# Three mixed inputs' last addition on GpSimd, first products split by token halves, and constants' transfers in the plan of an RWKV-6 block

## The chip, the cores and the metric

The kernel runs on one core of a Trainium2 chip. The metric is the device time in microseconds of one execution, from the runs without a profiler; one further execution was profiled, and all rows below come from it. A core has five engines that run beside each other, each in the order of its own instruction queue: TensorE (PE, matrix products into PSUM), VectorE (DVE), ScalarE (ACT), GpSimd (POOL) and SyncE (SP, which here issues most DMAs).

## The reference

One RWKV-6 block over x of shape (32, 128, 512): batch 32, 128 tokens, 512 channels, 32 heads of 16. Cut to what matters:

```python
xn = ln(x)*ln1_w + ln1_b
sx = previous_token(xn) - xn
xxx = tanh((xn + sx*maa_x) @ maa_w1)            # 512 -> 5 x 32
xxx = matmul(xxx.reshape(b, l, 5, 1, 32), maa_w2)  # each 32 -> 512
x5 = xn + sx*(maa_stack + xxx)                  # five mixed inputs
w = exp(-exp(time_decay + tanh(x5[1] @ decay_w1) @ decay_w2))  # 512 -> 64 -> 512
r, k, v = x5[3] @ Wr.T, x5[0] @ Wk.T, x5[2] @ Wv.T
g = silu(x5[4] @ Wg.T)
# per head and token: out = r . (u*k*v + s);  s = k*v + w*s
x = x + (group_norm(out) * g) @ Wo.T
# second half: ln, token shift, x + sigmoid(xr @ Wr2.T) * (relu(xk @ Wk2.T)**2 @ Wv2.T)
```

All of it is fp32.

## The kernel before

The batch is cut into 8 groups of 4 sequences, so that a group has N = 512 token columns; channels stand in four slices of 128 partitions (NE = 4). For each group the work is written as several Python generators, each a stream of instructions in order:

- `front_mix`: load x, layer norm and transposition (`layernorm_T`), the first product with `maa_w1` (`pm` for inputs 0 to 3, 128 weight columns; `pm2` for input 4), tanh, and for each of five inputs m the products with `maa_w2` (`side_by_side`) and the mixing (`mixed`): one instruction that adds `maa_stack` and multiplies by sx (L453), and one that adds xn (L455), for each of the four slices.
- `front_proj`: the decay product `pd` with `decay_w1` (L489), its tanh (L492), the decay w, and the projections k, r, v, each from one mixed input. `front_gate` makes the gate from input 4.
- `prep` and the `rec_*` streams: the recurrence. For each of 34 steps per group, 32 of them go through POOL (product L689, pair sum L693), DVE (scan L711, product with r L713) and PE (accumulation by transposing products L746). The two others need neither POOL nor the scan.
- `back`: group norm, output projection, second layer norm and the feed-forward part. The last group's `back` runs as two halves (`last1`, `last2`).

No stream waits in Python for the hardware. A planner (`Plan`) draws up one order for all engines ahead of time: each `yield Op(engine, us, ...)` states what the next instructions cost, what they read, write and allocate, and the planner picks, among the streams whose next Op could start within `EPSILON` of the earliest, the one with the earliest due time. A stream's due times run evenly from v0 to v1 over its steps, both from the table `DUE`, with the group's number added. The instructions are then issued in that order, so that an engine's queue holds instructions of several groups, and an instruction whose operands come late holds up everything behind it on its engine. The hardware's own semaphores secure the data; costs and due times only set the order. `xfer` is the planned transfer time on an issuing engine's queue; `port=True` says that an instruction takes the port that DVE and POOL share.

The products with few weight columns: `pm2` multiplies 96 columns of `w1_sb`, of which the middle 32 are zero and the last 32 a copy of the first, so that one tanh (L445) fills both halves of `thb` that `side_by_side` reads with two 64-row weights at once. `pd` likewise has the 64 decay columns twice. The copies are made on POOL in group 0 (L427, L428).

`constants()` issues the small loads at the start of group 0: `vec`, `pv`, `w1_sb`, `w2p`, `dw1_sb`, `dw2p` and `u_sb`, on SP's and ACT's queues, and four small POOL instructions that wait for `vec`. The planner knows nothing of them. The PSUM tiles named `ps` have four buffers, for all streams.

Of the kernel before, what the change touches and what calls it, by code (L numbers as in the profile page):

```python
# [8 lines left out]
F32 = mybir.dt.float32  # L9
I32 = mybir.dt.int32  # L10
AF = mybir.ActivationFunctionType
ALU = mybir.AluOpType
AX = mybir.AxisListType

P = 128
B, L, E = 32, 128, 512
H, S = 32, 16
NE = E // P
HE = P // S
GB = 4  # L20
NG = B // GB
N = GB * L
# [19 lines left out]
WINDOW, KEEP, WAKE = 3.41, 0.4, 0.7  # L42
LANDING = 2.0
HOP = (0.2, 0.05, 0.05, 0.04, 0.08)
EPSILON = 0.0397


DUE = {"rec": (-0.0, 1.1), "mix": (-1.199, -0.678), "proj": (-1.193, 1.513), "gate": (1.096, 1.348), "prep": (0.06, 0.276), "back": (1.128, 2.553), "last1": (-13.962, -9.529), "last2": (6.538, 25.524)}


class Buf:
# [130 lines left out]
def rwkv6_block(ctx: ExitStack, tc: tile.TileContext, x, prev, s0, vecs, u, maa_w1, maa_w2,  # L182
# [44 lines left out]
    u_sb = const.tile([P, S], F32, name="u_sb")  # L227


    w1_sb = const.tile([P, NE, 7 * XM], F32, name="w1_sb")  # L230
    w2p = const.tile([P, 5, E // 2], F32, name="w2p")
    dw1_sb = const.tile([P, NE, 2, XD], F32, name="dw1_sb")
    dw2p = const.tile([P, E // 2], F32, name="dw2p")
    thb = Buf(const.tile([P, N], F32, name="thb"))
    ident = const.tile([P, P], F32, name="ident")
# [4 lines left out]
                          ident.rearrange("p (b h e) -> p b e h", b=GB, e=NE))  # L240
    nc.gpsimd.memset(mhalf, -0.5)
    nc.gpsimd.memset(thb.t, 0.0)
    nc.gpsimd.memset(w1_sb[:, :, 5 * XM : 6 * XM], 0.0)
    nc.vector.memset(w2p, 0.0)

    def constants():
        nc.sync.dma_start(out=vec, in_=vecs)
        nc.gpsimd.tensor_scalar(ffn[:, 0, :], vec[:, V_FK, :], -1.0, 1.0, ALU.mult, ALU.add)
        nc.gpsimd.tensor_scalar(ffn[:, 2, :], vec[:, V_FR, :], -1.0, 1.0, ALU.mult, ALU.add)
        nc.gpsimd.tensor_tensor(ffn[:, 1, :], ffn[:, 0, :], vec[:, V_LN2B, :], ALU.mult)  # L250
        nc.gpsimd.tensor_tensor(ffn[:, 0, :], ffn[:, 0, :], vec[:, V_LN2W, :], ALU.mult)
        nc.sync.dma_start(out=pv, in_=prev)
        halves = lambda w, h: w.rearrange("r (f h p) -> h r f p", h=2, p=P)[h]
        nc.sync.dma_start(out=w1_sb[:, :, 0 : 5 * XM], in_=maa_w1.rearrange("(c p) o -> p c o", p=P))
        for m in (1, 0, 2, 3, 4):
            for h, queue in enumerate((nc.sync, nc.scalar)):
                r = h * XD + (XM if m in (1, 3) else 0)
                queue.dma_start(out=w2p[r : r + XM, m, :].rearrange("r (f p) -> r f p", p=P),
                                in_=halves(maa_w2[m * XM : (m + 1) * XM, :], h))
            if m == 1:  # L260
                nc.sync.dma_start(out=dw1_sb[:, :, 0, :], in_=decay_w1.rearrange("(c p) o -> p c o", p=P))
                for h, queue in enumerate((nc.sync, nc.scalar)):
                    queue.dma_start(out=dw2p[h * XD : (h + 1) * XD, :].rearrange("r (f p) -> r f p", p=P),
                                    in_=halves(decay_w2, h))
        for e in range(NE):
            nc.sync.dma_start(out=lanes(u_sb, e), in_=u[e * HE : (e + 1) * HE, :].unsqueeze(0).to_broadcast([GB, HE, S]))
# [6 lines left out]
    def col(v, e):  # L273
        return vec[:, v, e : e + 1]

    def bt(ap):
        return ap.rearrange("p (b t) -> p b t", t=L)
# [106 lines left out]
    def row(xnT, e, shift, bs=range(GB)):  # L384

        return xnT[:, e * GB + bs[0] : e * GB + bs[-1] + 1, shift : shift + L]

    def matmuls(p, w, xin, e, cols=slice(0, N)):
        for c in range(NE):
            nc.tensor.matmul(p, lhsT=w[:, c, e * P : (e + 1) * P], rhs=xin[:, c, cols], start=(c == 0), stop=(c == NE - 1))  # L390

    def side_by_side(pp, w, up, low):

        for p, h, t in zip(pp, (slice(0, XD), slice(XD, P)), (up, low)):
            nc.tensor.matmul(p.t, lhsT=w[h, :], rhs=t[h, :], start=True, stop=True)  # L395
# [11 lines left out]
    def front_mix(g, d):  # L407

        xt = yield from load_x(g, (lambda: "x1" in data[g - 3]) if g > 2 else (lambda: "xin" in data[0]) if g else None)
        if g == 0:  # L410
            constants()
        need = (lambda: "ln2" in data[g - 3]) if g > 2 else None
        def use(xnT, e, pt, tiles):

            yield Op(ACT, 0.75, w=[(pt, None)])
            nc.scalar.activation(pt.t, pt.t, AF.Identity, bias=col(V_LN1B, e), scale=col(V_LN1W, e))
            sx, xin = tiles
            yield Op(DVE, 0.69, r=[(xnT, e), (xnT, "p"), (pt, None)], w=[(sx, e)])
            nc.vector.tensor_tensor(bt(sx[:, e, :]), row(xnT, e, 0), bt(pt.t), ALU.subtract)
            yield Op(DVE, 0.75, r=[(pt, None), (sx, e)], w=[(xin, e)], end=[pt])  # L420
            nc.vector.scalar_tensor_tensor(xin[:, e, :], sx[:, e, :], col(V_MAAX, e), pt.t, ALU.mult, ALU.add)

        xnT, sx, xin = yield from layernorm_T(g, xt, None, V_LN1W, V_LN1B, 0, use, ("sx", "mx"), need)
        d["xin"] = True
        if g == 0:
            yield Op(POOL, 0.9)
            nc.gpsimd.tensor_copy(w1_sb[:, :, 6 * XM : 7 * XM], w1_sb[:, :, 4 * XM : 5 * XM])  # L427
            nc.gpsimd.tensor_copy(dw1_sb[:, :, 1, :], dw1_sb[:, :, 0, :])  # L428
        (pm,) = yield Op(PE, 8 * PASS, r=[(xin, None)], w=[(0, None)], alloc=["ps"])
        for c in range(NE):  # L430
            nc.tensor.matmul(pm.t, lhsT=w1_sb[:, c, 0 : 4 * XM], rhs=xin[:, c, :], start=(c == 0), stop=(c == NE - 1))
        (pm2,) = yield Op(PE, 8 * PASS, r=[(xin, None)], w=[(0, None)], alloc=["ps"], end=[xin])
        for c in range(NE):
            nc.tensor.matmul(pm2[0 : 3 * XM, :], lhsT=w1_sb[:, c, 4 * XM : 7 * XM], rhs=xin[:, c, :],
                             start=(c == 0), stop=(c == NE - 1))
        (tha,) = yield Op(ACT, 0.6, r=[(pm, None)], w=[(0, 0)], alloc=["tha"])
        nc.scalar.activation(tha[:, 0, :], pm.t, AF.Tanh)

        yield Op(ACT, 0.6, r=[(pm, None)], w=[(tha, 1)])
        nc.scalar.activation(tha[0:XD, 1, :], pm[XD:P, :], AF.Tanh)  # L440
        yield Op(ACT, 0.6, r=[(pm, None)], w=[(tha, 2)], end=[pm])
        nc.scalar.activation(tha[XD:P, 1, :], pm[0:XD, :], AF.Tanh)
        yield Op(ACT, 0.6, r=[(pm2, None)], w=[(thb, None)], end=[pm2],
                 need=(lambda: "mixed" in data[g - 1]) if g else None)
        nc.scalar.activation(thb[0 : 3 * XM, :], pm2[0 : 3 * XM, :], AF.Tanh)  # L445

        done = [0, 0]

        def mixed(m, i, pp, x5):

            for f, p in zip((2 * i, 2 * i + 1), pp):
                yield Op(DVE, 0.75, r=[(p, None), (sx, None)], w=[(p, None)])
                nc.vector.scalar_tensor_tensor(p.t, p.t, col(V_MAA + m, f), sx[:, f, :], ALU.add, ALU.mult)  # L453
                yield Op(DVE, 0.69, r=[(p, None), (xnT, None)], w=[(x5, f)], end=[p])
                nc.vector.tensor_tensor(bt(x5[:, f, :]), bt(p.t), xnT[:, f * GB : (f + 1) * GB, 1 : L + 1], ALU.add)  # L455
                done[1] += 1
            if i == 1:
                d["x5", m] = x5

        for m in (1, 0, 3, 2, 4) if g else (1, 0, 2, 3, 4):  # L460
            up, low = (thb.t, thb.t) if m == 4 else (tha[:, 0, :], tha[:, 1, :]) if m < 2 else (tha[:, 1, :], tha[:, 0, :])
            for i in range(2):

                pp = yield Op(PE, PAIR, r=[(thb, None), (tha, None)], w=[(0, None), (1, None)],
                              alloc=["ps", "ps"] + ([] if i else ["mx"]), need=lambda: done[1] >= done[0] - 1)
                if i == 0:
                    x5 = pp.pop()
                side_by_side(pp, w2p[:, m, i * P : (i + 1) * P], up, low)
                done[0] += 2
                plan.add(mixed(m, i, pp, x5), plan.due, plan.due + 0.02, 4)  # L470
        yield Op(PE, 0.0, need=lambda: done[1] == 5 * NE)
        xnT.open = sx.open = tha.open = False
        d["mixed"] = True

    def front_proj(g, d):
# [8 lines left out]
            ws[3] = yield from weight(wr)  # L484
        yield Op(PE, 0.0, need=has(1))
        x5 = d["x5", 1]
        (pd,) = yield Op(PE, 8 * PASS, r=[(x5, None)], w=[(0, None)], alloc=["ps"], end=[x5])
        for c in range(NE):
            nc.tensor.matmul(pd.t, lhsT=dw1_sb[:, c, :, :].rearrange("p h o -> p (h o)"), rhs=x5[:, c, :],  # L489
                             start=(c == 0), stop=(c == NE - 1))  # L490
        (dlo,) = yield Op(ACT, 0.6, r=[(pd, None)], w=[(0, None)], alloc=["blk"], end=[pd])
        nc.scalar.activation(dlo.t, pd.t, AF.Tanh)  # L492
        for i in range(2):
            pp = yield Op(PE, PAIR, r=[(dlo, None)], w=[(0, None), (1, None)], alloc=["ps", "ps"], end=[dlo] if i else [])
            side_by_side(pp, dw2p[:, i * P : (i + 1) * P], dlo.t, dlo.t)
# [489 lines left out]
```

## Time and profile before

| | |
|---|---|
| runs without a profiler | 1593.56 us median of 3 (1592.97 to 1594.41) |
| profiled execution | 1598.86 us, span 1597.1 us |
| mean granted TensorE clock | 0.955 |
| instructions | 16306 |
| recurrence product on POOL (L689) | 256 times, 613.0 us |
| recurrence pair sum on POOL (L693) | 256 times, 271.5 us, mean 1061 ns |
| scan and product on DVE (L711, L713) | 256 times each, 313.0 and 312.9 us |
| mixing on DVE (L453, L455) | 160 times each, 120.2 and 110.3 us |
| decay product (L489) | 64 records, 33.6 us |
| first product of input 4 (L434) | 64 records, 28.8 us |
| tanh of these (L492, L445) | 8 times each, 4.8 and 4.7 us |

The span is the time from the first instruction to the last; around it lie 1.8 us that the profiled execution's own time has besides. Each fp32 matmul of the program leaves two records on PE. Their mean durations are latencies: matmuls overlap, and a record of 512 columns follows the one before it by 0.43 us. Busy time of an engine is the union of its instructions' times.

### The profile page before, as it was taken

Reading aid. Unit: us, or ns where it says so; the run is one execution under the profiler, and the core shown is the slowest. Engines: PE = TensorE matmul, PEld = TensorE weight load, DVE = VectorE, ACT = ScalarE, POOL = GpSimd, SP = SyncE. Lnnn points to the kernel's source line nnn. Section 1 sums busy time; section 2 is a strip of 40 time slices with the busy share of each in tenths; the row PEclk is TensorE's granted clock in tenths of the full one; section 3 lists DMA queues with packets and bytes.
Section 4 is the critical chain, followed back from the end, with each engine's and each line's share of the span. In section 5 each row is a group of like instructions: output and inputs, shape, how many; then the busy total and the mean of one; then the engine's idle time right before and its main releaser. Section 6 shows DMA issues by size and latency. Waiting matters only on the chain.

```text
span 1597.1 us, 16306 instructions
## 1 busy us (share of the span) xinstructions
PE 1448.0 (91%) x5216; PEld 753.9 (47%) x5216; DVE 1325.2 (83%) x1702; ACT 641.2 (40%) x1229; POOL 913.8 (57%) x551
## 2 busy tenths in 40 slices
PE   4898797789999999999999999999999999987878
PEld 1334354344554454544555355544555454545444
DVE  4537999988999799987999799997999999788642
ACT  4223233433443444433444345433444344336243
POOL 3007575676765475844676375844766576778300
PEclk8799799989999999999999999999999999998989
DMA  6120222142314233233413324042422324150130
GB/s 214 36 83 24 93 73 66 61 134 86 119 44 141 90 99 109 73 116 102 126 50 115 110 80 132 32 144 86 132 70 82 123 77 121 49 176 5 59 120 27
DMA packets 127559, 146.86 MB, mean 92 GB/s; under 512 B 8177, under 2 KB 77297, under 8 KB 126449
## 3 DMA queue, kind: packets, MB, share of 16 engines
q1 hardware_dynamic: 92112, 128.81, 24.6%
q10 hardware_dynamic: 35360, 17.02, 3.8%
q8 instruction: 41, 0.67, 0.2%
q14 instruction: 46, 0.37, 0.1%
HBM read 94.41 MB, written 17.83 MB: 70 GB/s over the span
## 4 chain that ended last, share of the span: by engine, by line
PE 58%; DVE 28%; POOL 5%; issue 5%; DMA 3%; ACT 1%; SPq 1%; DVEq 0%; ACTq 0%; POOLq 0%
PE ps L390 24%; PE acc L746 8%; PE ps L834 7%; PE ps L395 6%; PE ps L908 5%; PE ps L924 5%; DVE sc L711 5%; DVE rm L713 4%; POOL am L689 3%; DVE ps L453 2%; DVE ps L619 2%; DVE mx L455 2%; POOL a L693 2%; PE ps L489 1%; DVE rk L627 1%
## 5 line engine op out<-in xcount | busy, mean ns | idle before, releaser
L689 POOL TENSOR_TENSOR am<-v,k 128x1024 f32<-128x1024 f32 x256 | 613.0, 2394 | 97.7 <-DMA r<-blk 77.7
L390 PE MATMUL ps<-mx,wt 128*128 128x512 f32 (+1 forms) x1312 | 586.5, 595 | 26.0 <-DVE rk L627 10.2
L693 POOL TENSOR_TENSOR a<-am 128x504 f32<-128x504 f32 x256 | 271.5, 1061 | 427.1 <-DVE sc L711 407.2
L390 PEld LDWEIGHTS ps<-mx,wt 128*128 128x128 f32 x1312 | 243.6, 193 | 303.6 <-issue 261.7
L713 DVE TENSOR_TENSOR rm<-sc,r 128x1024 f32<-128x1024 f32 x256 | 312.9, 1222 | 43.0 <-PE acc L746 31.7
L746 PE MATMUL acc<-by_head,rm 128*128 128x128 f32 x2176 | 281.7, 278 | 38.5 <-DVE rm L713 28.0
L711 DVE TENSOR_TENSOR_SCAN sc<-sc,a 128x512 f32<-128x512 f32 x256 | 313.0, 1223 | 4.0 <-POOL a L693 3.2
L746 PEld LDWEIGHTS acc<-by_head,rm 128*128 128x128 f32 x2176 | 249.8, 143 | 140.1 <-issue 66.5
L664 ACT COPY sc<-w 128x512 f32<-128x512 f32 x256 | 151.3, 591 | 233.3 <-DVE rm L713 196.5
L453 DVE SCALAR_TENSOR_TENSOR ps<-ps,vec,sx 128x512 f32<-128x512 f32 x160 | 120.2, 752 | 74.0 <-PE ps L395 73.0
L834 PE MATMUL ps<-wt,mx 128*128 128x512 f32 x256 | 128.9, 653 | 7.3 <-DVE mx L455 6.8
L395 PE MATMUL ps<-tha,w2p 64*128 64x512 f32 x256 | 97.2, 700 | 26.7 <-DVE mx L455 16.4
L675 ACT COPY a<-st 128x8 f32<-128x8 f32 x256 | 51.3, 202 | 166.1 <-DVE sc L711 145.6
L908 PE MATMUL ps<-wt,mx 128*128 128x512 f32 x256 | 115.1, 592 | 0.0
L455 DVE TENSOR_TENSOR mx<-ps,xnT 128x512 f32<-128x512 f32 x160 | 110.3, 691 | 5.3
L924 PE MATMUL ps<-wt,ev 128*128 128x512 f32 x224 | 101.3, 595 | 2.0 <-DVE rm L727 1.0
L525 ACT COPY blk<-ps 128x512 f32<-128x512 f32 x96 | 55.9, 583 | 94.1 <-PE ps L390 91.6
L834 PEld LDWEIGHTS ps<-wt,mx 128*128 128x128 f32 x256 | 51.2, 210 | 79.4 <-issue 63.5
L351 POOL TENSOR_TENSOR rstd<-rstd,mhalf 128x4 f32<-128x4 f32 (+1 forms) x17 | 17.1, 1003 | 99.0 <-DVE rstd L349 98.7
L908 PEld LDWEIGHTS ps<-wt,mx 128*128 128x128 f32 x256 | 46.8, 190 | 49.8 <-issue 49.7
L924 PEld LDWEIGHTS ps<-wt,ev 128*128 128x128 f32 x224 | 40.5, 190 | 44.3 <-issue 40.9
L395 PEld LDWEIGHTS ps<-tha,w2p 64*128 64x128 f32 x256 | 25.9, 198 | 73.4 <-DVE mx L455 35.3
(109 smaller groups left out, 1282.8 us busy)
## 6 DMA issues: line engine op xcount, KB each, us to landing
x<-in_x SPq DMA_DIRECT2D x15, 1024.0 KB
wt<-in_wk SPq DMA_DIRECT2D x8, 1024.0 KB
wt<-in_wr SPq DMA_DIRECT2D x8, 1024.0 KB
wt<-in_wg SPq DMA_DIRECT2D x8, 1024.0 KB
dgate<-blk SPq DMA_DIRECT2D x32, 256.0 KB
wt<-in_wo SPq DMA_DIRECT2D x8, 1024.0 KB
wt<-in_fk SPq DMA_DIRECT2D x8, 1024.0 KB
wt<-in_fr SPq DMA_DIRECT2D x8, 1024.0 KB
```

What stands on the lines that cost most here:

```text
L390: nc.tensor.matmul(p, lhsT=w[:, c, e * P : (e + 1) * P], rhs=xin[:, c, cols], start=(c == 0), stop=(c == NE - 1))
L395: nc.tensor.matmul(p.t, lhsT=w[h, :], rhs=t[h, :], start=True, stop=True)
L453: nc.vector.scalar_tensor_tensor(p.t, p.t, col(V_MAA + m, f), sx[:, f, :], ALU.add, ALU.mult)
L664: nc.scalar.copy(sc.t, d["w01"][:, q : q + 1, :].to_broadcast([P, DH, T2]))
L689: nc.gpsimd.tensor_tensor(am.t, v[:, ds, :], k[:, q : q + 1, :].to_broadcast([P, DH, L]), ALU.mult)
L693: nc.gpsimd.tensor_tensor(a[:, :, 1:T2], am2[:, :, 0 : T2 - 1, 0], am2[:, :, 0 : T2 - 1, 1], ALU.add)
L711: nc.vector.tensor_tensor_scan(scf, scf, a.t.rearrange("p d n -> p (d n)"), 0.0, ALU.mult, ALU.add)
L713: nc.vector.tensor_tensor(pair(rm.t), sc.t.unsqueeze(3).to_broadcast([P, DH, T2, 2]), r2[:, q : q + 1, :, :].to_broadcast([P, DH, T2, 2]), ...
L746: nc.tensor.matmul(acc[:, i, :], lhsT=rm[:, i, :], rhs=by_head, is_transpose=True, start=(q == 0 and i % 4 == 0), stop=(q == S), skip_grou ...
L834: nc.tensor.matmul(p.t, lhsT=att[:, c, b * L : (b + 1) * L], rhs=wot[:, c, :], start=(c == 0), stop=(c == NE - 1))
L908: nc.tensor.matmul(p.t, lhsT=xr[:, c, b * L : (b + 1) * L], rhs=frt[:, c, :], start=(c == 0), stop=(c == NE - 1))
L924: nc.tensor.matmul(p2.t, lhsT=kv[:, c, b * L : (b + 1) * L], rhs=fvt[:, c, :], start=(c == 0), stop=(c == NE - 1))
```

## The change

Three parts, and new due times for all streams.

1. In groups 1 to 7, for the inputs m = 2, 3, 4, DVE's first mixing instruction writes straight to the mixed input in SBUF and gives the PSUM buffer back, and the last addition runs on POOL, in place.
2. `pm2` and `pd` no longer carry their weight columns twice. The tokens are cut into two halves of 256; both use the same weights, and the second half's product goes to PSUM partitions 64 and up (`first_split`). Four tanh instructions (`in_both_halves`) then write each half to both row halves of the target. The POOL copies and the zero columns go.
3. Ahead of `constants()` stand two Ops without instructions of their own, so that the plan counts the constants' issue and transfer times on SP and ACT.

```diff
+ON_POOL = (2, 3, 4)
-EPSILON = 0.0397
+EPSILON = 0.0388
-DUE = {"rec": (-0.0, 1.1), "mix": (-1.199, -0.678), "proj": (-1.193, 1.513), "gate": (1.096, 1.348), "prep": (0.06, 0.276), "back": (1.128, 2.553), "last1": (-13.962, -9.529), "last2": (6.538, 25.524)}
+DUE = {"rec": (0.171, 1.108), "mix": (-4.67, -2.417), "proj": (-4.683, 4.311), "gate": (0.588, 0.608), "prep": (-4.19, 1.684), "back": (-0.012, 3.928), "last1": (-21.388, 9.796), "last2": (10.392, 13.665)}
...
-    w1_sb = const.tile([P, NE, 7 * XM], F32, name="w1_sb")
+    w1_sb = const.tile([P, NE, 5 * XM], F32, name="w1_sb")
-    dw1_sb = const.tile([P, NE, 2, XD], F32, name="dw1_sb")
+    dw1_sb = const.tile([P, NE, XD], F32, name="dw1_sb")
-    nc.gpsimd.memset(w1_sb[:, :, 5 * XM : 6 * XM], 0.0)
...
+    def first_split(p, w, rows, xin):
+        for c in range(NE):
+            for h in range(2):
+                nc.tensor.matmul(p[h * XD : h * XD + rows, 0 : N // 2], lhsT=w[:, c, :],
+                                 rhs=xin[:, c, h * N // 2 : (h + 1) * N // 2], start=(c == 0), stop=(c == NE - 1))
+
+    def in_both_halves(t, p, rows):
+        for h in range(2):
+            for k in range(2):
+                nc.scalar.activation(t[k * XD : k * XD + rows, h * N // 2 : (h + 1) * N // 2],
+                                     p[h * XD : h * XD + rows, 0 : N // 2], AF.Tanh)
...
         if g == 0:
+            yield Op(SP, 5.5, xfer=4.0)
+            yield Op(ACT, 3.9)
             constants()
...
-        if g == 0:
-            yield Op(POOL, 0.9)
-            nc.gpsimd.tensor_copy(w1_sb[:, :, 6 * XM : 7 * XM], w1_sb[:, :, 4 * XM : 5 * XM])
-            nc.gpsimd.tensor_copy(dw1_sb[:, :, 1, :], dw1_sb[:, :, 0, :])
...
-        (pm2,) = yield Op(PE, 8 * PASS, r=[(xin, None)], w=[(0, None)], alloc=["ps"], end=[xin])
-        for c in range(NE):
-            nc.tensor.matmul(pm2[0 : 3 * XM, :], lhsT=w1_sb[:, c, 4 * XM : 7 * XM], rhs=xin[:, c, :],
-                             start=(c == 0), stop=(c == NE - 1))
+        (pm2,) = yield Op(PE, 2 * PAIR, r=[(xin, None)], w=[(0, None)], alloc=["ps"], end=[xin])
+        first_split(pm2, w1_sb[:, :, 4 * XM : 5 * XM], XM, xin)
...
-        yield Op(ACT, 0.6, r=[(pm2, None)], w=[(thb, None)], end=[pm2],
+        yield Op(ACT, 1.6, r=[(pm2, None)], w=[(thb, None)], end=[pm2],
                  need=(lambda: "mixed" in data[g - 1]) if g else None)
-        nc.scalar.activation(thb[0 : 3 * XM, :], pm2[0 : 3 * XM, :], AF.Tanh)
+        in_both_halves(thb, pm2, XM)
...
+                if g and m in ON_POOL:
+                    yield Op(DVE, 0.75, r=[(p, None), (sx, None)], w=[(x5, f)], end=[p])
+                    nc.vector.scalar_tensor_tensor(x5[:, f, :], p.t, col(V_MAA + m, f), sx[:, f, :], ALU.add, ALU.mult)
+                    yield Op(POOL, 1.08, r=[(xnT, None)], w=[(x5, f)], port=True)
+                    nc.gpsimd.tensor_tensor(bt(x5[:, f, :]), bt(x5[:, f, :]), row(xnT, f, 1), ALU.add)
+                else:
+                    yield Op(DVE, 0.75, r=[(p, None), (sx, None)], w=[(p, None)])
...
-        (pd,) = yield Op(PE, 8 * PASS, r=[(x5, None)], w=[(0, None)], alloc=["ps"], end=[x5])
-        for c in range(NE):
-            nc.tensor.matmul(pd.t, lhsT=dw1_sb[:, c, :, :].rearrange("p h o -> p (h o)"), rhs=x5[:, c, :],
-                             start=(c == 0), stop=(c == NE - 1))
-        (dlo,) = yield Op(ACT, 0.6, r=[(pd, None)], w=[(0, None)], alloc=["blk"], end=[pd])
-        nc.scalar.activation(dlo.t, pd.t, AF.Tanh)
+        (pd,) = yield Op(PE, 2 * PAIR, r=[(x5, None)], w=[(0, None)], alloc=["ps"], end=[x5])
+        first_split(pd, dw1_sb, XD, x5)
+        (dlo,) = yield Op(ACT, 1.6, r=[(pd, None)], w=[(0, None)], alloc=["blk"], end=[pd])
+        in_both_halves(dlo, pd, XD)
```

The DMA lines in `constants()` change only in their targets, `w1_sb` and `dw1_sb` as a whole, with the same bytes. PASS is 0.43 and PAIR 2.45 x PASS, as before.

More of the change, by code (lines that the diff above doesn't have):

```diff
@@ L253, in constants @@
         halves = lambda w, h: w.rearrange("r (f h p) -> h r f p", h=2, p=P)[h]
-        nc.sync.dma_start(out=w1_sb[:, :, 0 : 5 * XM], in_=maa_w1.rearrange("(c p) o -> p c o", p=P))
+        nc.sync.dma_start(out=w1_sb, in_=maa_w1.rearrange("(c p) o -> p c o", p=P))
         for m in (1, 0, 2, 3, 4):
@@ L260, in constants @@
             if m == 1:
-                nc.sync.dma_start(out=dw1_sb[:, :, 0, :], in_=decay_w1.rearrange("(c p) o -> p c o", p=P))
+                nc.sync.dma_start(out=dw1_sb, in_=decay_w1.rearrange("(c p) o -> p c o", p=P))
                 for h, queue in enumerate((nc.sync, nc.scalar)):
@@ L451, in mixed @@
             for f, p in zip((2 * i, 2 * i + 1), pp):
[L452 to L455, printed above, removed]
+                if g and m in ON_POOL:
[5 more added lines that the diff above has]
+                    yield Op(DVE, 0.75, r=[(p, None), (sx, None)], w=[(p, None)])
+                    nc.vector.scalar_tensor_tensor(p.t, p.t, col(V_MAA + m, f), sx[:, f, :], ALU.add, ALU.mult)
+                    yield Op(DVE, 0.69, r=[(p, None), (xnT, None)], w=[(x5, f)], end=[p])
+                    nc.vector.tensor_tensor(bt(x5[:, f, :]), bt(p.t), row(xnT, f, 1), ALU.add)
                 done[1] += 1
```

## The prediction

> **What bounds the kernel now.** I read the page's engine totals first, then the chain of waits, then stretches of it.
>
> ```profile
> PE 1448.0 (91%) x5216; PEld 753.9 (47%) x5216; DVE 1325.2 (83%) x1702; ACT 641.2 (40%) x1229; POOL 913.8 (57%) x551
> ...
> PE 58%; DVE 28%; POOL 5%; issue 5%; DMA 3%; ACT 1%; SPq 1%; DVEq 0%; ACTq 0%; POOLq 0%
> ```
>
> TensorE (PE) is the bound, VectorE (DVE) a close second: the chain that ends last runs 58% through PE and 28% through DVE. GpSimd (POOL) has 683 us idle in all and carries 5% of the chain. The windows view says where:
>
> ```profile
> 150.00:350.00 200.00, 166.87 (x610) 87.36 (x610) 184.91 (x227) 65.11 (x129) 131.68 (x77) 0.90 0.25 80
> 350.00:1400.00 1050.00, 1008.21 (x3762) 527.34 (x3761) 949.24 (x1187) 451.05 (x865) 663.50 (x388) 0.99 0.30 97
> ...
> 880.92:1062.58 181.66, 174.17 (x649) 90.77 (x649) 164.68 (x209) 78.78 (x150) 112.65 (x66) 0.99 0.31 99
> ```
>
> Columns: stretch, its length, busy PE, weight loads, DVE, ScalarE (ACT), POOL, then PE's granted clock. From 150 to 350 us DVE is the bound (185 of 200), from 350 to 1400 PE is (1008 of 1050). One group there takes 182 us (the stretch from one decay product, L489, to the next). In that period the chain goes through PE except in two DVE runs, 956 to 972 us and 1030 to 1059 us.
>
> **First products (pm2, L434; pd, L489).** The rows the sum uses, from the groups kept apart by shape (count | busy us, mean ns | idle before):
>
> ```profile
> L746 PE MATMUL acc<-by_head,rm 128*128 128x128 f32 x2176 | 281.7, 278 | 38.5 <-DVE rm L713 28.0 <-DVE rm L727 6.7 <-ACT y L760 3.6
> ...
> L455 DVE TENSOR_TENSOR mx<-ps,xnT 128x512 f32<-128x512 f32 x160 | 110.3, 691 | 5.3
> ...
> L489 PE MATMUL ps<-mx,dw_sb 128*128 128x512 f32 x64 | 33.6, 675 | 4.0 <-DVE rk L627 4.0
> ...
> L395 PE MATMUL ps<-blk,dw2p 64*128 64x512 f32 x64 | 19.4, 635 | 1.3 <-ACT blk L492 0.8 <-DVE mx L455 0.5
> ...
> L898 ACT ACTIVATE k<-ps 128x256 f32<-128x256 f32 x8 | 3.0, 378 | 5.9 <-PE ps L390 5.9
> ```
>
> The means are latencies; PE pipelines. Eight records of one product take 3.43 us in the chain (880.92 us), 0.43 us each. Now each product becomes 8 matmuls (16 records) of 256 columns, with the two token halves in different column groups of the array. Full-width 256-column records follow each other at 0.22 us (24 in 5.42 us at 1551.76 us), so with no overlap 16 take 3.45 us: no gain. With perfect overlap it is 1.72 us. The nearest row for overlap is L395, two 64-row products side by side: 4 records in 1.06 us where perfect overlap is 0.86, so 0.2 us is exposed per pair. Scaled to half the columns, four pairs take 2.1 us; with the 0.2 us kept whole, 2.5 us. I take 2.3: **-1.1 us per product**, 16 products, **-18 us** of PE work.
>
> A rule speaks against it. The Trainium skill, "TensorE: Matmul & The Clock Gate", section "Part 3: Packing small matmuls", says that weight loads overlap running matmuls only when the row group differs; token halves in column groups share all rows. L395 packs rows, so it does not test that. By L746, eight 128-column loads and their matmuls take 0.875 us, so a load costs at most 0.11 us per 128 columns: 0.03 us for 32 columns, 0.055 us for 64 (estimates). By that rule the products take 3.9 and 4.3 us: +0.5 and +0.9 us, +11 us in all. But the same section lists three column tiles at 2.38 times the speed (no run here shows it), so I stay with L395's cost.
>
> Of the 18 us, PE's share of the chain is on the path: 0.58 x 18 = **-10.5 us** (ends: -16, all overlap perfect, and +6.5).
>
> Each product's tanh becomes four ACT instructions over 32 or 64 rows x 256: 4 x 0.38 (L898) = 1.52 us, plus gaps, against 0.6. That is +0.96 us, 15 us in all. ACT has 103 of 182 us free in a period and 1% of the chain, and the 1.1 us taken from PE offsets the latency: **0** (ends 0 and +15, if each time PE waits for the tanh; PE now waits 4.6 us in all for L492). The PSUM buffer of pm2 stays taken about 0.9 us longer, in the same term.
>
> **Additions to POOL.** In groups 1 to 7, three of five inputs x four slices: 84 adds leave DVE, 84 x 0.691 = -58 us. L455 is 2.0% of the chain (32 us for 160 adds), so 84 of them are 17 us of path; the cross-check 0.28 x 58 gives 16. **-17 us** (ends 0 and -58). The first DVE instruction then writes SBUF and frees PSUM 0.7 us sooner; that helps L395, which waits for L455 60 us in all, and is not counted again.
>
> POOL gets 84 x 1.08 (L693's 1.061 us for 504 columns, scaled to 512) = +91 us. The Trainium skill, "GPSIMD Engine Reference", section "4.1 Engine selection", says elementwise adds belong on VectorE, GpSimd being about twice as slow with two inputs. Here the ratio is 1.08/0.69 = 1.56. By the rule the move costs 84 x 0.69 = 58 us of engine time, by the rows 33 us; but either lands on an engine with 5% of the chain: 0.05 x 91 = **+4.5 us** (ends 0 and +91).
>
> Behind a waiting add in POOL's queue stands the recurrence's next product (L689, 2.39 us), for whose sum (L693) the scan on DVE waits. The add also comes up to 2.39 us late if it is behind that product, and PE's projections r, v and gate wait for it: 21 times, 0.4 to 2.8 us. PE has other groups' products to run; it waits 20 us in all for L455 at L390 today. **+2 us** (ends 0 and +59).
>
> DVE reads of two SBUF tensors stretch beside POOL work: L619 takes 1.42 us on average, 0.68 at best. With L723 that is 35 us of waiting; POOL goes from 57% to 63% busy, so +3.5 us, on the path 28%: **+1 us**.
>
> **Constants and the start.** From the timeline (start, duration, engine, line, and in brackets the idle time before and what ended it):
>
> ```profile
> 6.55 0.19 POOL L248 TENSOR_SCALAR ffn<-vec 128x4 f32<-128x4 f32 x1 [4.16 <-DMA vec<-in_vecs]
> ...
> 30.22 0.69 DVE L331 BATCH_NORM_STATS2 stats<-x 128x6 f32<-128x512 f32 x1 [8.21 <-DMA x<-in_x]
> ...
> 36.48 0.57 ACT L445 ACTIVATE thb<-ps 96x512 f32<-96x512 f32 x1
> ...
> 37.11 2.07 PE L395 MATMUL ps<-tha,w2p 64*128 64x512 f32 x2 [8.58 <-ACT thb L445]
> ...
> 38.91 0.75 DVE L453 SCALAR_TENSOR_TENSOR ps<-ps,vec,sx 128x512 f32<-128x512 f32 x1
> ```
>
> The planner put the next groups' statistics ahead of group 0's mixing, since it thought x had come; DVE stood 8.2 us for it, and ACT's last tanh (L445) and PE behind it. PE's first pairs end at 28.5 us, DVE mixes at 38.9: 10.4 us lost. With the constants' 5.5 and 4.0 us on SP's books the plan should mix first. Against it: the new due times put mix at -4.614 and proj at -4.558 at first, and after the x load mix at -4.5574, proj at -4.5581. So the 1 MB of wv is issued ahead of vec in SP's queue. Three such loads landed within 9.9 us (20.3 to 30.2), 3.3 us each, so vec comes at 9.9 us, POOL's four ffn instructions end at 10.7 instead of 7.4, and group 0's rstd behind them starts at 10.7, not 9.68, 1 us late. pv and w1 come later too, but are used only from 13.8 us. wv itself is there sooner, which helps its centring on POOL and x behind it. **-8 us** (ends -10.4 and +3). The two weight copies (0.7 us of POOL) and a memset (0.2) go; other waits hide them: 0.
>
> **Order.** All due times change. What that does elsewhere no row shows; one misjudged transfer costs about 10 us (the start), so ends -10 and +10, value 0. The tail from 1501 us has none of the moved work.
>
> **Sum**: -10.5 - 17 + 4.5 + 2 + 1 - 8 = **-28 us**. The profiled execution took 1598.9 us (span 1597.1), 5.3 above the median of the runs, so 1571, or **1566 us** as a median.
>
> **Rivals.**
> - *More of the relief counts.* PE's own work per period, from the rows: 32 products at 3.44, three first products 10.3, 12 pairs at 1.06, 34 steps at 0.875, 12 transposes at 0.44 = 168 us of 182. The room is there. All of 18, 58 and 8 us, less the 7.5 us added: -77, 1517 us; half-way to it 1540. Against: one period has only 7.5 us of PE idle. Chance 0.10.
> - *The column halves do not overlap*: +6.5 for -10.5, so 1583 us; with some DVE relief lost too, no change. For: the rule above. Chance 0.12, of which 0.05 within 0.2%.
> - *POOL becomes the bound (slower).* At 229 to 247 and 329 to 346 us the chain is POOL's product and sum, one step per 3.55 us. A group's 12 adds are 13 us, 3.7 such steps. Once about 40% of the 91 us lie on the path, the 35.5 us of gains are gone; at 55%, +14.5, 1608 us; at all, 1649. For: POOL runs in order, and each add waits for DVE. Against: POOL waits 407 us for the scan, and 15 of 20 mixing slices of the period lie at 885 to 941 us, where PE leads. Chance 0.18.
> - The forecast as worked out, 1541 to 1580 us: 0.60.
>
> **Range.** 1535 to 1600 us holds the forecast, the no-overlap case and the low end of the POOL case, and the half-way point of the large gain; the likeliest case's own range is 1541 to 1580. Faster by over 0.2% (about what a measurement of this kernel can tell from no change) 0.77, within it 0.05, slower 0.18.
>
> **What would show it.** Right: 16 records of a split product within 2.5 us; DVE about 8 us less busy per period and POOL 13 more; the first mixing near 29 us; periods of 178 or 179 us. Wrong: 16 records in 3.4 us or more (columns); POOL's share of the chain above 10%, or L693 waiting on the new adds; vec's lateness passing to PE's first product; periods of 182 us with DVE idle grown, which would say that the order, not work, sets the pace.

## The result and the profile after

The changed kernel takes **1535.54 us** (median of 4 runs, 1535.00 to 1536.44) against 1593.99 in the runs beside it: ratio 0.9629, 95% interval 0.961 to 0.9647. That is 58 us less, just over twice the 28 forecast. The profiled execution has a span of 1533.2 us (before: 1597.1) at a mean granted TensorE clock of 0.959 (0.955).

Engine totals and the chain of waits of the kernel after:

```profile
PE 1410.0 (92%) x5344; PEld 746.6 (49%) x5344; DVE 1270.9 (83%) x1618; ACT 656.2 (43%) x1277; POOL 1024.8 (67%) x632
...
PE 51%; DVE 27%; POOL 13%; issue 6%; DMA 2%; ACT 1%; SPq 1%; DVEq 0%; POOLq 0%; ACTq 0%
```

PE is busy 38 us less, DVE 54 less, POOL 111 more. POOL's share of the chain rose from 5 to 13%, which the forecast had named as a mark of trouble, and yet the time fell. The stretches (same columns as before), the last one group:

```profile
150.00:350.00 200.00, 180.78 (x670) 94.05 (x671) 172.06 (x195) 68.31 (x139) 149.89 (x96) 0.92 0.29 91
350.00:1400.00 1050.00, 1007.40 (x3983) 543.10 (x3982) 949.31 (x1183) 489.08 (x951) 800.44 (x479) 0.98 0.31 101
...
810.30:980.60 170.30, 167.89 (x667) 88.76 (x665) 156.11 (x198) 80.34 (x156) 129.94 (x78) 1.00 0.33 106
```

A group takes 170.3 us instead of 182 (forecast: 178 or 179), of which PE is idle 2.4 instead of 7.5. Work on DVE is down 8.6 us per group, about the 12 additions at 0.69, as forecast; work on POOL is up 17.3, where 13 were forecast. Between 150 and 350 us DVE no longer leads. The rows of what moved, by shape:

```profile
L708 POOL TENSOR_TENSOR a<-am 128x504 f32<-128x504 f32 x256 | 286.1, 1118 | 201.5 <-DVE sc L726 181.1 <-ACT a L690 5.9 <-ACT blk L515 0.5
L467 POOL TENSOR_TENSOR mx<-mx,xnT 128x512 f32<-128x512 f32 x84 | 99.7, 1198 | 40.9 <-DVE mx L465 40.3
...
L397 PE MATMUL ps<-mx,dw_sb 128*64 128x256 f32 x128 | 17.5, 419 | 0.8 <-DVE mx L472 0.8
L397 PE MATMUL ps<-mx,w_sb 128*32 128x256 f32 x128 | 15.4, 382 | 0.0
```

An addition on POOL takes 1198 ns, not 1080, and POOL stands 40 us for the DVE instruction ahead of it. The latencies of L397 say little of the pace; the timeline does (604.81 us, columns as before):

```profile
604.81 1.44 PEld L397 LDWEIGHTS ps<-mx,w_sb 128*32 128x32 f32 x16 [0.76 <-PE ps L444]
604.81 1.92 PE L397 MATMUL ps<-mx,w_sb 128*32 128x256 f32 x16
```

Sixteen records in 1.92 us (1.95 for the decay product from 449 us on) are 0.12 each, where full-width records of that length follow at 0.22: the column halves overlap all but fully (perfect overlap is 1.72). The start:

```profile
11.87 1.02 POOL L352 TENSOR_TENSOR rstd<-rstd,mhalf 128x4 f32<-128x4 f32 x1
...
30.18 0.69 DVE L332 BATCH_NORM_STATS2 stats<-x 128x6 f32<-128x512 f32 x1 [3.95 <-DMA x<-in_x]
...
37.51 0.75 DVE L470 SCALAR_TENSOR_TENSOR ps<-ps,vec,sx 128x512 f32<-128x512 f32 x1
```

The statistics of the next groups still stand ahead of group 0's mixing and still wait for x, until 30.18 us (before: 30.22). The first mixing comes at 37.5 us, not at 29 as forecast.

### The profile page after: what moved, and what is told of

It reads as the page before. It is cut to its first block, busy times and chain, and to the rows that moved or that the text cites. A ratio compares the mean times of both kernels' runs of the same rounds, so it can differ in the third digit from the quotient of the medians.

```text
span 1533.2 us, 16578 instructions
## 1 busy us (share of the span) xinstructions
PE 1410.0 (92%) x5344; PEld 746.6 (49%) x5344; DVE 1270.9 (83%) x1618; ACT 656.2 (43%) x1277; POOL 1024.8 (67%) x632
## 4 chain that ended last, share of the span: by engine, by line
PE 51%; DVE 27%; POOL 13%; issue 6%; DMA 2%; ACT 1%; SPq 1%; DVEq 0%; POOLq 0%; ACTq 0%
PE ps L391 18%; PE acc L761 8%; POOL am L704 7%; PE ps L939 6%; PE ps L923 6%; PE ps L410 6%; DVE sc L726 5%; POOL a L708 4%; DVE rm L728 4%; PE ps L849 2%; DVE rk L642 2%; DVE ps L634 2%; PE ps L397 2%; PE ps L444 2%; DVE ps L470 1%
## 5 line engine op out<-in xcount | busy, mean ns | idle before, releaser
L704 POOL TENSOR_TENSOR am<-v,k 128x1024 f32<-128x1024 f32 x256 | 610.3, 2384 | 88.7 <-DMA r<-blk 70.4
L708 POOL TENSOR_TENSOR a<-am 128x504 f32<-128x504 f32 x256 | 286.1, 1118 | 201.5 <-DVE sc L726 181.1
L761 PE MATMUL acc<-by_head,rm 128*128 128x128 f32 x2176 | 290.8, 283 | 36.0 <-DVE rm L728 29.9
L467 POOL TENSOR_TENSOR mx<-mx,xnT 128x512 f32<-128x512 f32 x84 | 99.7, 1198 | 40.9 <-DVE mx L465 40.3
L923 PE MATMUL ps<-wt,mx 128*128 128x512 f32 x256 | 115.7, 595 | 0.0
L849 PE MATMUL ps<-wt,mx 128*128 128x512 f32 x256 | 112.8, 598 | 0.6 <-DVE rk L642 0.6
L410 PE MATMUL ps<-tha,w2p 64*128 64x512 f32 x256 | 89.1, 677 | 18.0 <-DVE mx L472 12.0
L352 POOL TENSOR_TENSOR rstd<-rstd,mhalf 128x4 f32<-128x4 f32 (+1 forms) x17 | 20.2, 1191 | 120.1 <-DVE rstd L350 120.1
L470 DVE SCALAR_TENSOR_TENSOR ps<-ps,vec,sx 128x512 f32<-128x512 f32 x76 | 57.3, 753 | 36.7 <-PE ps L410 36.3
L465 DVE SCALAR_TENSOR_TENSOR mx<-ps,vec,sx 128x512 f32<-128x512 f32 x84 | 61.8, 743 | 21.8 <-PE ps L410 21.7
```

The lines of the kernel that those rows point to most:

```text
L467: nc.gpsimd.tensor_tensor(bt(x5[:, f, :]), bt(x5[:, f, :]), row(xnT, f, 1), ALU.add)
L704: nc.gpsimd.tensor_tensor(am.t, v[:, ds, :], k[:, q : q + 1, :].to_broadcast([P, DH, L]), ALU.mult)
L708: nc.gpsimd.tensor_tensor(a[:, :, 1:T2], am2[:, :, 0 : T2 - 1, 0], am2[:, :, 0 : T2 - 1, 1], ALU.add)
L761: nc.tensor.matmul(acc[:, i, :], lhsT=rm[:, i, :], rhs=by_head, is_transpose=True, start=(q == 0 and i % 4 == 0), stop=(q == S), skip_grou ...
L849: nc.tensor.matmul(p.t, lhsT=att[:, c, b * L : (b + 1) * L], rhs=wot[:, c, :], start=(c == 0), stop=(c == NE - 1))
L923: nc.tensor.matmul(p.t, lhsT=xr[:, c, b * L : (b + 1) * L], rhs=frt[:, c, :], start=(c == 0), stop=(c == NE - 1))
```

## The experiments

The question was which part brings the 58 us, and whether the new due times bring any by themselves. Undoing a part and drawing up the order anew mixes the two. So most runs keep **the changed kernel's order to the instruction** and change only which engine does a piece of work, or whether POOL waits. The table has medians of 4 runs (10 for before_hold and tuned_old_work) in us, with the ratio to the kernel before, run beside them, and its 95% interval.

| run | what differs | median | ratio |
|---|---|---|---|
| fix_dve | after's order, 84 additions on DVE, POOL neither adds nor waits | 1604.0 | 1.0063 (1.004–1.0086) |
| fix_serial | after's order, weight columns twice as before | 1550.84 | 0.9727 (0.9705–0.975) |
| fix_both | both of these | 1621.85 | 1.017 (1.0151–1.0188) |
| fix_dve_m4 | only input 4's 28 additions on DVE | 1580.31 | 0.9909 (0.9884–0.9933) |
| fix_noadd | the 84 additions on no engine, no wait on POOL | 1559.05 | 0.978 (0.9759–0.9801) |
| fix_gate | POOL's additions cut to 8 of 512 columns, waits kept | 1534.46 | 0.9635 (0.9608–0.9661) |
| fix_dve_hold | fix_dve, with POOL's waits kept by a tiny instruction | 1563.41 | 0.9811 (0.9782–0.984) |
| const_first | constants issued ahead of wv's load | 1535.08 | 0.963 (0.9611–0.9648) |
| const_alone | before, with the constants' Ops | 1605.6 | 1.0076 (1.0053–1.0099) |
| before_hold | before, with a tiny POOL instruction behind each of the 84 | 1593.2 | 1.0003 (0.999–1.0017) |
| tuned_old_work | before's work, constants' Ops, due times redrawn for it | 1594.5 | 1.0016 (1.0001–1.0031) |
| tuned_pool_only | after without the split, due times redrawn for it | 1580.03 | 0.9916 (0.9899–0.9933) |
| tuned_all | after, due times redrawn once more | 1537.83 | 0.9652 (0.9638–0.9667) |

### One part undone in the same order

fix_dve (the plan still books the addition on POOL; DVE does it through PSUM as before):

```diff
-    nc.vector.scalar_tensor_tensor(x5[:, f, :], p.t, col(V_MAA + m, f), sx[:, f, :], ALU.add, ALU.mult)
+    nc.vector.scalar_tensor_tensor(p.t, p.t, col(V_MAA + m, f), sx[:, f, :], ALU.add, ALU.mult)
+    nc.vector.tensor_tensor(bt(x5[:, f, :]), bt(p.t), row(xnT, f, 1), ALU.add)
-    nc.gpsimd.tensor_tensor(bt(x5[:, f, :]), bt(x5[:, f, :]), row(xnT, f, 1), ALU.add)
```

> The changed kernel in its own planned order (due times and costs in the plan as changed), but the 84 last additions are issued on VectorE again, straight after the first mixing instruction and through PSUM as before; only the hardware's work differs. VectorE gets 58 us of work back, GpSimd loses some 100. Theory 'work, at its share of the chain' (the prediction's -17 + 7.5): about +10 us on 1535.5, so 1545. Theory 'work, in full' (the changed kernel's period of 170 us is possible only because VectorE was relieved): +30 to +50, so 1565 to 1585. Theory 'order' (the new due times and the constants in the plan brought the gain): within 5 us of 1535.5.

fix_serial (`pm2` and `pd` as before: weights twice, one matmul of 512 columns per slice, one tanh; `w1_sb`, `dw1_sb` and POOL's copies as before):

```diff
-    first_split(pd, dw1_sb, XD, x5)
+    for c in range(NE):
+        nc.tensor.matmul(pd.t, lhsT=dw1_sb[:, c, :, :].rearrange("p h o -> p (h o)"), rhs=x5[:, c, :], start=(c == 0), stop=(c == NE - 1))
-    in_both_halves(dlo, pd, XD)
+    nc.scalar.activation(dlo.t, pd.t, AF.Tanh)
```

> The changed kernel in its own planned order, but the decay product and the first product of input 4 carry their weight columns twice again (one 512-column matmul per slice, one tanh), with the two small copies on GpSimd at the start. TensorE gets 16 x 1.5 us = 24 us of work back, ScalarE loses 15. Theory 'work, at its share of the chain': +14 us, so 1549. 'Work, in full' (TensorE is the bound throughout): +24, so 1560. 'Order': within 5 us of 1535.5.

fix_both joins the two edits.

> Both of the above at once, in the changed kernel's planned order: the engines do the work of the kernel before, and only the order and the constants' place are the changed kernel's. 'Work, at its share of the chain': about 1559. 'Work, in full': 1585 to 1610, that is about the kernel before or slower. 'Order': within 10 us of 1535.5.

The split is worth 15.3 us (1550.84 less 1535.54), or 17.9 where DVE adds (1621.85 less 1604.0). The move of the additions is worth 68.5 us (1604.0 less 1535.54), **more than the 58 us of work that leave DVE**. The two together, 86.3, are more than the whole gain: with before's work on the engines, after's order costs 28.4 us against before's own. So something other than DVE's work is in the 68.5.

### What the additions' move is made of

fix_noadd drops the POOL line and nothing else. fix_dve_m4 puts input 4 alone back on DVE:

```diff
+    late = m not in (4,)
-    nc.vector.scalar_tensor_tensor(x5[:, f, :], p.t, col(V_MAA + m, f), sx[:, f, :], ALU.add, ALU.mult)
+    nc.vector.scalar_tensor_tensor(x5[:, f, :] if late else p.t, p.t, col(V_MAA + m, f), sx[:, f, :], ALU.add, ALU.mult)
+    if not late:
+        nc.vector.tensor_tensor(bt(x5[:, f, :]), bt(p.t), row(xnT, f, 1), ALU.add)
```

> The changed kernel in its own order without the 84 last additions on any engine (xn is left out of inputs 2, 3 and 4 in groups 1 to 7). GpSimd loses 100 us of work, and the projections no longer wait for it. The prediction priced GpSimd's side at +7.5 us (4.5 for its time, 2 for lateness, 1 for the shared port): then about 1528. If GpSimd's additions are hidden: 1533 to 1536. If GpSimd has become a bound (its share of the chain went from 5% to 13%): -20 us or more, under 1516.

> The changed kernel in its own order, with only the 28 additions of input 4 back on VectorE (19 us of the 58), through PSUM. fix_dve cost +68 us for 84. If VectorE's work counts in full and in proportion: +20 to +25, so 1556 to 1560. If the cost in fix_dve is a disorder that a few displaced instructions cause (their place in the queue, not their time): well over +30 or near +5, out of proportion.

With the additions on no engine at all the kernel is **23.5 us slower** (1559.05) than with 100 us of them on POOL. Work was taken away, and time was added. And 28 of the additions put back cost 44.8 us, over twice their 19.4 us of DVE work. Both runs also take POOL's wait away: an addition in POOL's queue waits for the DVE mixing instruction, and holds the recurrence's next product (L704) behind it. The forecast had this wait as a cost. The timeline shows what it does. DVE and then POOL of the kernel after, in a group norm:

```profile
839.82 1.07 DVE L815 SCALAR_TENSOR_TENSOR th<-th 128x128 f32<-128x128 f32 x1
840.93 0.29 DVE L816 SCALAR_TENSOR_TENSOR th<-th 128x128 f32<-128x128 f32 x1
841.25 0.29 DVE L814 TENSOR_TENSOR th<-th 128x128 f32<-128x128 f32 x1
...
842.89 0.29 DVE L816 SCALAR_TENSOR_TENSOR th<-th 128x128 f32<-128x128 f32 x1
843.10 0.74 DVE L465 SCALAR_TENSOR_TENSOR mx<-ps,vec,sx 128x512 f32<-128x512 f32 x1
```

```profile
839.72 1.02 POOL L708 TENSOR_TENSOR a<-am 128x504 f32<-128x504 f32 x1
843.92 1.18 POOL L467 TENSOR_TENSOR mx<-mx,xnT 128x512 f32<-128x512 f32 x1 [3.18 <-DVE mx L465]
845.06 2.36 POOL L704 TENSOR_TENSOR am<-v,k 128x1024 f32<-128x1024 f32 x1
```

and the same place in fix_noadd (lines one lower), again DVE, then POOL:

```profile
849.37 2.31 DVE L814 SCALAR_TENSOR_TENSOR th<-th 128x128 f32<-128x128 f32 x1
851.72 1.07 DVE L815 SCALAR_TENSOR_TENSOR th<-th 128x128 f32<-128x128 f32 x1
852.83 2.40 DVE L813 TENSOR_TENSOR th<-th 128x128 f32<-128x128 f32 x1
855.26 0.29 DVE L814 SCALAR_TENSOR_TENSOR th<-th 128x128 f32<-128x128 f32 x1
```

```profile
849.10 2.44 POOL L703 TENSOR_TENSOR am<-v,k 128x1024 f32<-128x1024 f32 x1
851.62 1.03 POOL L707 TENSOR_TENSOR a<-am 128x504 f32<-128x504 f32 x1
852.73 2.35 POOL L703 TENSOR_TENSOR am<-v,k 128x1024 f32<-128x1024 f32 x1
```

Each long DVE instruction ends within 0.2 us of the POOL instruction beside it: a Newton step of the group norm's reciprocal root (L813 to L815; 0.29 us in the kernel after, where nothing runs beside it) takes 2.3 us if a recurrence product runs. In the kernel after, POOL stands 3.18 us at the addition, and seven steps go by at 0.29 us each.

The next two runs test whether it is the wait. fix_gate keeps every wait and cuts the addition to 8 of 512 columns; fix_dve_hold is fix_dve with a tiny POOL instruction behind DVE's:

```diff
-    nc.gpsimd.tensor_tensor(bt(x5[:, f, :]), bt(x5[:, f, :]), row(xnT, f, 1), ALU.add)
+    nc.gpsimd.tensor_tensor(x5[:, f, 0:8], x5[:, f, 0:8], xnT[:, f * GB, 1:9], ALU.add)
```

```diff
     nc.vector.tensor_tensor(bt(x5[:, f, :]), bt(p.t), row(xnT, f, 1), ALU.add)
+    nc.gpsimd.tensor_scalar(x5[:, f, 0:8], x5[:, f, 0:8], 1.0, None, ALU.mult)
```

> The changed kernel in its own order, with each of the 84 additions on GpSimd cut to 8 of 512 columns (xn is left out of the other columns of inputs 2, 3 and 4 in groups 1 to 7). GpSimd's queue keeps all its waits for VectorE, but 75 to 90 of the 100 us of additions go. In fix_noadd, where the waits went too, the time rose by 23.5 us, and VectorE's two-input instructions stretched in other places. Theory 'hold': the additions held GpSimd's queue back and so kept its long products off VectorE's small instructions; the time comes back to 1530 to 1540. Theory 'time': what mattered was when GpSimd ran, which shifts here as well; 1550 to 1560.

> The changed kernel in its own order, with the 84 additions on VectorE (as in fix_dve) and GpSimd's waits kept: where the addition stood, GpSimd multiplies 8 of its columns by 1. Against fix_gate (1534.5) it differs by VectorE's 58 us alone. Chain share (the prediction's step): +17, 1551. VectorE's work in the proportion that fix_dve - fix_noadd showed (0.77): +45, 1580. In full: +58, 1593. Hold of no use once VectorE is loaded: as fix_dve, 1604.

It is the wait: putting it back, with next to no work on POOL, brings the time down in both cases. All four runs have after's order and split:

| | POOL waits | POOL doesn't | the wait is worth |
|---|---|---|---|
| no addition on DVE | 1534.46 | 1559.05 | 24.6 |
| 84 additions on DVE | 1563.41 | 1604.0 | 40.6 |
| DVE's 58 us are worth | 28.9 | 45.0 | |

And POOL's own time for the additions, fix_gate against after, is worth 1.1 us (1535.54 less 1534.46), within the runs' scatter. Three rows each of fix_dve and fix_dve_hold, by shape:

```profile
L814 DVE TENSOR_TENSOR th<-th 128x128 f32<-128x128 f32 x21 | 18.7, 890 | 0.5
L815 DVE SCALAR_TENSOR_TENSOR th<-th 128x128 f32<-128x128 f32 x21 | 16.2, 774 | 0.7
L816 DVE SCALAR_TENSOR_TENSOR th<-th 128x128 f32<-128x128 f32 x21 | 10.0, 477 | 0.7
```

```profile
L815 DVE TENSOR_TENSOR th<-th 128x128 f32<-128x128 f32 x21 | 6.7, 319 | 0.5
L816 DVE SCALAR_TENSOR_TENSOR th<-th 128x128 f32<-128x128 f32 x21 | 6.1, 292 | 0.7
L817 DVE SCALAR_TENSOR_TENSOR th<-th 128x128 f32<-128x128 f32 x21 | 6.1, 292 | 0.7
```

The same steps take 44.9 us without the wait, 18.9 with it; in fix_noadd they take 44.9, in fix_gate 18.2. What that is worth can be read from DVE's totals, since fix_gate, after and fix_noadd give DVE the same 1618 instructions in the same order, and fix_dve_hold and fix_dve the same 1702 (profiled executions, us; idle is span less busy):

| | span | DVE busy | DVE idle |
|---|---|---|---|
| fix_gate | 1530.5 | 1247.9 | 282.6 |
| after | 1533.2 | 1270.9 | 262.3 |
| fix_noadd | 1554.5 | 1273.4 | 281.1 |
| fix_dve_hold | 1563.3 | 1301.7 | 261.6 |
| fix_dve | 1600.8 | 1326.8 | 274.0 |

From fix_gate to fix_noadd DVE is busy 25.5 us longer, all of it in the Newton steps (26.7 us), its idle time is the same to 1.5 us, and the span grows by 24.0. From fix_dve_hold to fix_dve it is busy 25.1 us longer, again in these steps (26.0), and stands idle 12.4 us more. So the stretched steps account for the wait's worth where DVE does not add, and for two thirds of it where DVE does.

But stretched instructions do not lengthen the kernel everywhere. From fix_gate to after, DVE is busy 23.0 us longer too, now beside POOL's additions, and the span grows by only 2.7, because DVE stands idle 20.3 us less. One place where it stands is L840, which multiplies by the gate and waits until that is loaded again (`blk<-dgate`). Its rows in the order of the table:

```profile
L840 DVE SCALAR_TENSOR_TENSOR mx<-ps,blk 128x512 f32<-128x512 f32 x28 | 18.7, 683 | 10.8 <-DMA blk<-dgate 9.1 <-ACT ps L838 1.7
L840 DVE SCALAR_TENSOR_TENSOR mx<-ps,blk 128x512 f32<-128x512 f32 x28 | 18.6, 681 | 1.4 <-ACT ps L838 1.4
L839 DVE SCALAR_TENSOR_TENSOR mx<-ps,blk 128x512 f32<-128x512 f32 x28 | 18.6, 683 | 23.7 <-DMA blk<-dgate 20.2 <-ACT ps L837 3.5
L841 DVE SCALAR_TENSOR_TENSOR mx<-ps,blk 128x512 f32<-128x512 f32 x28 | 18.7, 684 | 4.1 <-DMA blk<-dgate 3.9 <-ACT ps L839 0.2
L840 DVE SCALAR_TENSOR_TENSOR mx<-ps,blk 128x512 f32<-128x512 f32 x28 | 18.6, 683 | 24.6 <-DMA blk<-dgate 21.2 <-ACT ps L838 3.5
```

The pause before it goes from 10.8 us in fix_gate to 1.4 in after and 23.7 in fix_noadd, and from 4.1 in fix_dve_hold to 24.6 in fix_dve; in fix_noadd, whose idle time is that of fix_gate, other pauses are shorter by as much. No run moves the Newton steps alone away from POOL's products, so this division is read from the traces and was not tested.

The granted clock is a rival for a small part of it. It was 0.944 to 0.950 in fix_dve's runs and 0.959 to 0.961 in fix_dve_hold's, 0.950 to 0.958 in fix_noadd's and 0.956 to 0.960 in fix_gate's. Among the runs of fix_serial the two at 0.966 are 4.7 us shorter than the two at 0.957; on that scale the clock makes some 5 us of the 40.6 and 3 of the 24.6 (estimates). Whether it is a cause or follows from the slower course, the runs do not say.

### The order, the constants and the start

const_first calls `constants()` ahead of the two Ops, so that vec is issued before the 1 MB of wv; const_alone adds the two Ops to the kernel before. before_hold adds the tiny POOL instruction of fix_dve_hold to the kernel before, behind the same 84 additions.

```diff
         if g == 0:
+            constants()
             yield Op(SP, 5.5, xfer=4.0)
             yield Op(ACT, 3.9)
-            constants()
```

```diff
         if g == 0:
+            yield Op(SP, 5.5, xfer=4.0)
+            yield Op(ACT, 3.9)
             constants()
```

> The changed kernel, but the constants' transfers are issued ahead of wv's load on SyncE's queue, with the same plan. In the changed kernel's trace group 0's rstd starts 2.2 us later than before and TensorE's first product 4.2 us later. If this lateness reaches the end: -3 to -4 us, 1532. If the next x, which lands at 30.2 us in both kernels, sets the start: within 1.5 us of 1535.5.

> The kernel before with the constants' two Ops in the plan, its own old due times and work. The prediction gave this part -8 us (the stall of 8.2 us for x at the start, and what stood behind it). If that holds: about 1585. If the stall only moves (x lands at 30.2 us in the changed kernel too, and VectorE's first mixing came at 37.5 us, not 29): 1590 to 1596. If due times that were drawn up without these Ops no longer fit: slower than 1600.

> The kernel before, its own order, with a small GpSimd instruction (8 columns times 1) behind each of the 84 mixing additions of inputs 2, 3 and 4 in groups 1 to 7, in GpSimd's queue and without a place in the plan. If a hold on GpSimd's queue during the mixing is worth something by itself: 5 to 25 us faster than 1593.5. If it was worth something only in the order drawn up with it: no change or slower, 1593 to 1620, since the recurrence's products stand behind it.

In const_first group 0's rstd starts at 9.81 us, not 11.87, and PE's first product at 11.94, not 16.10; but x lands at 30.0 us and the statistics are first again, and the time is the same. The constants' Ops alone, under before's due times, cost 12 us. The wait of POOL brings nothing in before's order (1593.2): there the same Newton steps already take 0.29 us on average. Of the two orders, only the one that sets POOL's products beside DVE's small steps gains by the wait.

In the last three runs the due times were redrawn, for the work that the kernel then has:

```diff
-DUE = {"rec": (-0.0, 1.1), "mix": (-1.199, -0.678), "proj": (-1.193, 1.513), ...
+DUE = {"rec": (-0.002, 1.075), "mix": (-1.238, -0.675), "proj": (-1.201, 1.849), ...
```

> The kernel before, its work on all engines unchanged, with the constants' two Ops in the plan and due times drawn anew for just that work. It measures what order and constants are worth without any relief. Prediction's share: -8 for the constants, 0 for order, 1585. Theory 'work': no better than 1585. Theory 'order': under 1570, so that half or more of the 58 us need no change of work.

> The changed kernel without the split products (weight columns twice, one tanh each), with due times drawn anew for it. Against fix_serial (1550.8, same work in the changed kernel's order). If the split is worth its work at TensorE's share: within 10 us of 1551. The due times found here were not searched as long, so a longer time says little; a shorter one would say that part of fix_serial's +15 was order.

> The changed kernel with due times refined further for its own work, nothing else. If the plan's order is carried over to the chip closely: 3 to 5 us faster than 1535.5. If small shifts between plan and chip (the shared port above all) outweigh that: anywhere from -5 to +25 us.

With before's work, constants in the plan and due times of its own the kernel takes 1594.5: planning the constants and redrawing the order gain nothing by themselves here. How far this carries is shown by tuned_pool_only: it does the work of fix_serial in an order drawn up for that work and takes 1580.0, 29 us longer than fix_serial in after's order, though its due times were not searched for as long. The plan sees no stretching on DVE; that the shared port makes the difference between those two orders was not tested. One redrawn order is one sample. tuned_all, redrawn once more for the changed kernel's own work, is 2.3 us slower than it. No run that does all the work beat the changed kernel by more than 0.5 us (const_first).

## Why the forecast was half the gain

The path from before (1593.5) to after in runs that differ by one part each: +28.4 (after's order with before's work, fix_both), -17.9 (split, fix_dve), -40.6 (POOL's wait, fix_dve_hold), -28.9 (DVE's relief, fix_gate), +1.1 (POOL's time, after). The sum is -58. In another order of the steps the wait counts 24.6 and the relief 45.0. Beside the forecast's terms, POOL's wait is 43 us off (-40.6 for +2), DVE's relief 12 (-28.9 for -17), the first products 7, and order and constants together 36 the other way (+28.4 for -8). That the total is only 30 us off is in part luck: the largest two errors nearly cancel. Point by point:

- **First products, -10.5: mechanism right, a term mis-sized.** "I take 2.3: -1.1 us per product": a product takes 1.92 us, so -1.5, and 16 of them are 24 us of PE work, not 18. The weight 0.58 fits: it gives -14, and fix_serial measures -15.3, fix_both -17.9, both with the four tanh instructions on ACT in them. The rule that spoke against (the Trainium skill, "TensorE: Matmul & The Clock Gate", section "Part 3: Packing small matmuls": weight loads overlap only with another row group) would have given 3.9 us for 16 records; the trace has 1.92, with the 16 weight loads inside that time, and the measurement decides. What the four tanh instructions took back no run separates.
- **DVE's relief, -17: the weighing failed.** "L455 is 2.0% of the chain (32 us for 160 adds), so 84 of them are 17 us of path; the cross-check 0.28 x 58 gives 16." The 58 us were right (DVE is busy 54 less); they are worth 28.9 with POOL's wait and 45.0 without, 0.50 and 0.78 of the work, where the forecast took 0.28. (In the 28.9 is also that fix_dve_hold gives each PSUM buffer back one instruction later; no run separates it.) A likely reason, not tested: the chain names one engine at a time; where PE and DVE hand work to each other and PE has 7.5 us of idle time per group, a us off DVE also shortens steps that the chain books on PE.
- **POOL's wait, +2: the sign was wrong.** "Behind a waiting add in POOL's queue stands the recurrence's next product (L689, 2.39 us), for whose sum (L693) the scan on DVE waits." The queueing is as described; its worth is a gain of 25 to 41 us in this order. The held product was early: without the wait POOL then stands 356 us at L708 for the scan (fix_dve), with it 188 (fix_dve_hold). The step asked only who waits for POOL, not what POOL's running costs DVE: without the wait the Newton steps alone take 26 us more. The stretching was in the forecast as 3.5 us of DVE's time, and as a net sum that held (58 us of work left DVE, which is busy 54.3 less); what it had no term for is where the stretching falls.
- **POOL's time, +4.5: too much.** 99.7 us of additions cost about 1 us. The chain's share failed in the other direction here: 13% of the chain, and fix_gate, with 4%, is 1 us faster. The rival that POOL becomes the bound falls by this.
- **Constants and the start, -8: failed.** "With the constants' 5.5 and 4.0 us on SP's books the plan should mix first." It doesn't: statistics first, x as late as before. vec came even later than forecast (rstd at 11.87 us, not 10.7, and on to PE's first product), and that cost nothing (const_first). Why the plan still puts the statistics first was not tried.
- **Order, 0, ends -10 and +10: what it holds is larger.** Order and POOL's wait together are -12.2 (+28.4 - 40.6); apart, they are far outside these ends. The +28.4 hold the constants' Ops too; in before's order these alone cost 12 us (const_alone). The order is bad for before's work and good for the work and waits it was drawn up for.

The rival that ended nearest is "more of the relief counts" (1540 us at half-way, chance 0.10; half-way from 1566 to 1517 is in fact 1541.5, inside the forecast's own range). Its reason, that PE's and DVE's savings count nearly whole, holds for the split (15 to 18 of 24 us); for DVE it is half, and the rest of its size is the wait. The range, 1535 to 1600, holds the time at its edge, by half a microsecond.

Open: a version of before's work with POOL's wait in an order drawn up for it, which would say whether the wait needs the move of the additions at all; why input 4 makes two thirds of the loss in fix_dve_m4; what makes DVE stand 12 us longer in fix_dve than in fix_dve_hold; and whether the Newton steps alone, moved away from POOL's products, would bring what the wait brings.

## What to carry to other kernels

In this kernel, work taken from a second engine that is nearly always busy was worth more than its chain share and less than its whole duration, and the rising chain share of the receiving engine was no cost; price such a move between these ends. When an instruction is put into the queue of an engine that shares a port with another, ask not only who waits for what stands behind it, but what the held instruction would have slowed had it run at once. To judge the parts of a change to a planned kernel, keep the order fixed to the instruction and swap the work in it; and add a run with work removed but its waits kept, since a run without both mixes two effects of opposite sign.

## What was not expected of the hardware

- DVE's small instructions with two SBUF operands can stop for nearly the whole of a POOL instruction: 0.29 us becomes 2.3 to 2.4 us beside a product of 2.35 to 2.44. The Trainium skill, "SBUF — State Buffer", section "SBUF: two separate sides", states it as an exclusive lock that is held for a whole instruction, for a VectorE instruction with two SBUF inputs beside a GpSimd one that reads SBUF; the timelines agree.
- Two column halves of the array overlap fully enough to run 16 records of 256 columns in 1.92 us, with the 16 weight loads of 32 columns (1.44 us) inside that time.
- An addition of 128x512 takes 1198 ns on POOL where DVE takes 691, a ratio of 1.73; the 1061 ns of the pair sum, scaled, had given 1080. Moving 84 of them cost the receiving engine 99.7 us, DVE 23 us of longer instructions (fix_gate against after), and the kernel 1.
